# Two feed-forward layers on one core: the first product taken for pairs of batch elements in seven blocks of products

## The chip, the cores and the metric

The kernel runs on one NeuronCore of a Trainium2 chip, as one launch. The metric is the time of one execution on the device in microseconds (us); the time before is the median of five runs. All arithmetic is in 32-bit floats.

## The reference, cut to what matters

A sequence of two transformer blocks over 16 batch elements of 256 tokens with 256 features. Each block has a self-attention, a cross-attention and a feed-forward layer, each added to its input, with a layer norm modulated by a condition ahead of it. Only the feed-forward layers are changed:

```
# layer 0 (x: 16 x 256 x 256; ff_w1: 256 x 1024; ff_w2: 1024 x 256)
ffn_in = _adaln(x, cond, ln2_w, ln2_b, g2_w, g2_b, b2_w, b2_b)
h = jax.nn.gelu(ffn_in @ ff_w1 + ff_b1, approximate=False)
x = h @ ff_w2 + ff_b2 + x
# layer 1, the same with other weights
h = _ln(x, ln3_w, ln3_b) * (1 + sc3[:, None, :]) + sh3[:, None, :]
x = x + jax.nn.gelu(h @ W1 + b1, approximate=False) @ W2 + b2
```

Layer 0's attentions have 16 heads of 64 columns with rotary embedding, layer 1's 16 heads of 16 columns.

## The kernel before

There are six phases (self-attention, cross-attention and feed-forward of layer 0, then of layer 1) of 16 jobs, one for each batch element. An attention job has two steps `s`, a feed-forward job four. One loop over all steps issues everything; with `manual_schedule` the order in which the code issues is the order in which each engine (PE, DVE, ACT, POOL, and SP for the DMAs) works. An instruction that has to wait holds up everything behind it on its engine. PSUM is one tile, `banks`, of eight banks, and the code names the bank of each product.

A matrix product of 128 output rows is a call of `product` (line 82 in the profile): four matmuls of 32 output rows each, which lie on different columns of the array. Each such matmul instruction leaves two records in the profile.

**Preparing an input.** `prepare_moments` (mean and variance on DVE, lines 321 to 325, then `rstd` on POOL, line 327), `prepare_norm` (normalisation and 32x32 transposes on DVE, lines 335 and 345; four DMAs on SP that write `turned` to DRAM, line 350; then two bias additions on POOL, line 420), `prepare_fetch` (four DMAs that read `fetched` back transposed, line 360), `prepare_input` (`affine`: one half of the modulation on ACT, line 393, the other on POOL, line 394). These run one to three jobs ahead of the job that needs them.

**First product.** `ffn_hidden(job, u)` does a quarter of `ffn_in @ w1` in each of its four steps: two 128-row chunks of the 1024 hidden features, for each two products over the 256 input features and 256 tokens, so 16 products for each element, then two gelus on ACT straight from PSUM (line 701).

**Second product.** It is already done by Strassen's seven products. `fold_weights` (line 724, five additions of 128x512) makes sums of blocks of the second weight, once for each phase. `fold_inner` (line 733, five additions of 128x512) makes sums of blocks of the hidden values. `finish_folded` does seven products of 128x128 blocks over 512 features, 28 calls of `product` with 128 columns, into two banks, and adds them to `x` on DVE (lines 747 to 754). Folds of the element before come in step 0, its `finish_folded` in step 2. For layer 0's last elements, whose results are finished beside layer 1's first attention jobs, `finish` does the plain second product (addition on line 772). Layer 0's attentions end in the same folded way.

**Around the feed-forward phases.** The first job of a feed-forward phase also ends the last attention job: in layer 0 `sum_up` (sums of the softmax, reciprocal on line 609) and `scale` on POOL (line 624), in layer 1 `normalize` (reciprocal on line 677, shuffles on line 685, two multiplications on POOL, line 686) and `finish`. `fold_weights` comes in step 1 of this first job. At the end of the kernel the last element is folded and finished alone. `look_outside`, `judge` and `count_outside` read back all softmax sums, test their range and choose whether a general version has to run as well; on these inputs it does not.

Of the kernel before, what the change touches and what calls it, by code (L numbers as in the profile page):

```python
# [10 lines left out]
F32 = mybir.dt.float32  # L11
# [32 lines left out]
def fast(ctx: ExitStack, tc: tile.TileContext, a: dict, out: bass.AP, flag):  # L44
# [6 lines left out]
    assert NB >= 11  # L51
# [19 lines left out]
    turn_of_ffn = [1]  # L71

    def next_bank():
        turn_of_ffn[0] = (turn_of_ffn[0] + 1) % 8
        return turn_of_ffn[0]

    def product(out, lhsT, rhs, start, stop):


        for g in range(4):  # L80
            cut = slice(32 * g, 32 * g + 32)
            nc.tensor.matmul(out[cut], lhsT[:, cut], rhs, start=start, stop=stop)  # L82
# [307 lines left out]
    def affine(pt, cw, scale, bias, tag, name, eng=nc.gpsimd):  # L390

        dst = work.tile([cw, 2, N], F32, tag=tag, name=name)
        nc.scalar.activation(dst[:, 0, :], pt[:, 0, :], AF.Identity, bias=bias(0), scale=scale(0))
        eng.tensor_scalar(dst[:, 1, :], pt[:, 1, :], scale(1), bias(1), ALU.mult, ALU.add)
        return dst
# [41 lines left out]
    def prepare_input(job):  # L437

        b, key = job["b"], job["key"]
        factor, addend = job["phase"]["mod"]  # L440
        job["hT"] = hT = affine(
            job.pop("hraw"), P,
            lambda c: factor[:, c, b : b + 1], lambda c: addend[:, c, b : b + 1], "hT", f"hT_{key}",
            nc.vector if b == 0 and job["p"] == 0 else nc.gpsimd,
        )
        if not job["cross"]:
            job["kT"] = hT
        elif job["layer"] == 0:
            job["kT"] = affine(
                job.pop("craw"), P,  # L450
                lambda c: column("L0_xcond_ca_lnc_w", c), lambda c: column("L0_xcond_ca_lnc_b", c),
                "cT", f"cT_{key}",
            )
# [191 lines left out]
    def layer1_sums(job, c, e, at):  # L645

        key, v, prs = job["key"], job["v"], job["pr"].pop(2 * c + e)
        o = bank(at, N)
        for t in range(NT):
            for h in range(4):  # L650
                nc.tensor.matmul(  # L651
                    o[32 * h : 32 * h + 32], v[:, t, 4 * c + h, 32 * e : 32 * e + 32],
                    prs[h // 2][:, h % 2, t, :], start=(t == 0), stop=(t == NT - 1),
                )

        if c == 0 and e == 0:
            job["parts"].append(work.tile([P, 4, N], F32, tag="part", name=f"oT_{key}", bufs=4)[:, 0:2, :])
            job["sums"] = work.tile([P, N], F32, tag="inv", name=f"sums_{key}")  # L660
        raw, sums = job["parts"][0][:, c, :], job["sums"]
        if e == 0:
            nc.scalar.activation(raw, o, AF.Copy, scale=mask[:, 0:1])
        else:
            nc.vector.scalar_tensor_tensor(raw, o, mask[:, 1:2], raw, ALU.mult, ALU.add)
        eighth = mask[:, 4 - 2 * e + c : 5 - 2 * e + c]
        if c == 0 and e == 0:
            nc.scalar.activation(sums, o, AF.Copy, scale=eighth)
        else:
            nc.vector.scalar_tensor_tensor(sums, o, eighth, sums, ALU.mult, ALU.add)  # L670
# [17 lines left out]
    def ffn_hidden(job, u):  # L688
        w, key = job["phase"]["w"], job["key"]
        ph = bank(next_bank(), 2, N)  # L690
        if u % 2 == 0:
            job["halves"].append(work.tile([P, 4, N], F32, tag="part", name=f"g_{key}_{u}", bufs=4))
        g = job["halves"][-1][:, 2 * (u % 2) : 2 * (u % 2) + 2, :]
        for c in range(2):
            for k in range(KC):
                product(
                    ph[:, c, :], w[f"w1{u // 2}"][:, k, (2 * (u % 2) + c) * P : (2 * (u % 2) + c + 1) * P], job["hT"][:, k, :],
                    k == 0, k == KC - 1,
                )
        for c in range(2):  # L700
            nc.scalar.activation(g[:, c, :], ph[:, c, :], AF.Gelu, bias=column(w["b1"], 2 * u + c))  # L701
        job["parts"].append(g)
# [32 lines left out]
    def finish_folded(job, at):  # L735

        x, weights, hidden = xs[job["b"]], job["phase"]["folded"], job.pop("folded")
        hurry = len(at) == 3
        first, second, third = (bank(i, 4, P) for i in (at if hurry else (*at, at[1])))
        places = {5: first[:, 0], 2: first[:, 1], 4: first[:, 2], 3: first[:, 3],  # L740
                  1: third[:, 0], 7: second[:, 1], 6: second[:, 2]}
        for m in (3, 6, 4, 5, 2, 1, 7) if hurry else places:
            for c in range(4):
                product(places[m], hidden[m][:, c, :], weights[m][:, c, :], c == 0, c == 3)
# [8 lines left out]
        nc.vector.tensor_tensor(outer, third[:, 0:1, :].to_broadcast([P, 2, P]), outer, ALU.add)  # L753
# [22 lines left out]
    def look_outside():  # L776

        worst = const.tile([P, 2], F32, name="worst")
        every = wtile([P, 4 * NB * 16 * N // P], "wv", "every")
        nc.sync.dma_start(out=every, in_=sums_seen.rearrange("(p n) h r q -> p (n h r q)", p=4 * NB)  # L780
                          .rearrange("p (s m) -> (p s) m", s=P // (4 * NB)))
        return worst, every

    def judge(worst, every):
        nc.vector.tensor_reduce(worst[:, 0:1], every, AX.X, ALU.add)
        nc.vector.tensor_reduce(worst[:, 1:2], every, AX.X, ALU.min)
        nc.vector.tensor_scalar(within[:, 0:1], worst[:, 0:1], SUM_HIGH, None, ALU.is_le)
        nc.vector.tensor_scalar(within[:, 1:2], worst[:, 1:2], 1.0 / SUM_HIGH, None, ALU.is_ge)

    def count_outside():  # L790

        pw = bank(next_bank(), 2)[0:1]
# [107 lines left out]
    prepare_input(jobs[1])  # L900
    for i, (j, s) in enumerate(steps):
# [5 lines left out]
        late = prev if not ffn else jobs[j - 2] if prev["kind"] == "ffn" else None  # L907
# [4 lines left out]
        if s == 1 and job["b"] == (3 if ffn else 1) and more:  # L912
# [12 lines left out]
        if ffn and layer0 and job["b"] in (2, 5, 8):  # L925
            at = phases[3 + job["b"] // 3]
            if s == 0:
                at["make_mod"] = at["mod_load"]()
            if s == 3:
                make_mod = at  # L930
        if ffn and layer0 and job["b"] in (3, 6, 9) and s == 3:
            at = phases[2 + job["b"] // 3]
# [5 lines left out]
        if ffn:  # L938
            ffn_hidden(job, s)
            if s == 1 and prev["kind"] == "attn" and layer0:  # L940
                sum_up(prev, next_bank())
            if s == 2 and prev["kind"] == "attn" and not layer0:
                finish(prev, next_bank())
            if prev["kind"] == "ffn":
                if s == 0:
                    fold_inner(prev, nc.vector, 5, 2, 1, 7, 6)
                if s == 2:
                    finish_folded(prev, (next_bank(), next_bank()))
            then = attention(i + 2, 1)
            if s == 2 and then:  # L950
                stage_a(then[0], 0, next_bank())
            if s == 0 and prev["kind"] == "attn" and prev["layer"] == 1:
                normalize(prev)
            if late is not None and s == 3:
                finish(late, next_bank())
            if s == 2 and then:
                for t in range(NT):
                    layer1_values(then[0], next_bank(), t)
            if make_mod:
                make_mod["mod"] = make_mod["make_mod"](next_bank())  # L960
            if s == 1 and after is not None:
                prepare_fetch(after)
            if s == 1 and third is not None:
                prepare_moments(third)
                prepare_norm(third)
            if s == 1 and prev["kind"] == "attn":
                fold_weights(job["phase"])
            if s == 3 and after is not None:
                prepare_input(after)
            if s == 3 and prev["kind"] == "attn" and layer0:  # L970
                scale(prev)
        elif layer0:
            then = attention(i + 1, 0)
            stage_t(job, 2 * s, 0)
# [21 lines left out]
            if late is not None and s == 1:  # L996
                if then:
                    finish_folded(late, (4, 5))
# [12 lines left out]
            else:  # L1011
                prepare_norm(third)
                prepare_context(third)
                prepare_input(after)
                if job["b"] == 0:
                    fold_weights(job["phase"])
        else:
# [14 lines left out]
            if s == 0:  # L1032
                prepare_moments(third)
            else:
                prepare_norm(third)
                prepare_input(after)
        scores(i + 1)
        if job["last"] and s == 0 and job["b"] in (2, 6):
            seen_sums = look_outside() if job["b"] == 2 else count_outside()
        if job["last"] and s == 3 and job["b"] == 3:  # L1040
            judge(*seen_sums)
    fold_inner(jobs[-1], nc.vector, 6, 5, 2, 1, 7)
    finish_folded(jobs[-1], (1, 2, 3))
# [615 lines left out]
```

## Time and profile before

| | |
|---|---|
| median of five runs | 2200.36 us (2198.2 to 2200.98) |
| the profiled execution | 2201.28 us, span 2199.5 us |
| granted TensorE clock | 0.999 |
| PE busy | 2184.5 us (99%) |
| DVE busy | 1662.4 us (76%) |
| POOL busy | 1072.1 us (49%) |
| ACT busy | 839.1 us (38%) |
| feed-forward phase of layer 0 on PE | 1293.85 to about 1533 us |
| feed-forward phase of layer 1 on PE | 1982.2 to 2192 us |

A line of the profile's groups names the line of code, the engine, the operation, the output and input tiles, the shape and the count; then busy time in us and the mean of one instruction in ns; then the idle time of that engine just before, with what ended it. In a timeline the columns are the start and the duration in us, and the idle time before stands in brackets with what ended it. PEld is the loading of weights, which runs beside PE; SPq are the DMAs that SP issues. The records of matmuls overlap four deep, so the pace of PE is read from the starts of groups, not from the mean of one record. The slices of the page are a fortieth of the span, 55 us each.

### The profile page before, as it was taken

What the parts mean: (1) busy time and instruction counts of PE and PEld (TensorE: products, weight loads), DVE (VectorE), ACT (ScalarE), POOL (GpSimd) and SP (SyncE); (2) the same over time, 40 slices, a digit from 0 to 9 for tenths busy, and PEclk for the clock granted to TensorE, in tenths of its full rate; (3) what the DMA queues carried; (4) which work ended last, traced back from release to release, by engine and by line L of the source; (5) the groups of instructions that cost most, each with busy time, mean ns of one, the idle gap of its engine ahead of it and who ended that gap; (6) DMA issues with size and microseconds to landing.
All of it is one profiled execution on the core that took longest, in us unless ns stands there. A gap on an engine that the chain in (4) does not pass through costs nothing.

```text
span 2199.5 us, 110711 instructions
## 1 busy us (share of the span) xinstructions
PE 2184.5 (99%) x50469; PEld 1438.7 (65%) x50469; DVE 1662.4 (76%) x3119; ACT 839.1 (38%) x1306; POOL 1072.1 (49%) x1036
## 2 busy tenths in 40 slices
PE   9999999999999999999999999999999999999998
PEld 5666666666665666666666668786656556557887
DVE  5886777777788898889898876664777777777654
ACT  3323323323223323333333332334666666663322
POOL 3766656656657867676776752221323232222220
PEclk9999999999999999999999999999999999999999
DMA  6110111110132221212212033221222232223221
GB/s 192 46 39 22 25 40 23 24 41 22 27 85 72 68 63 35 55 46 43 57 36 60 23 74 87 52 45 29 62 42 42 55 92 59 62 52 85 61 63 36
DMA packets 307975, 117.78 MB, mean 54 GB/s; under 512 B 244308, under 2 KB 290728, under 8 KB 307368
## 3 DMA queue, kind: packets, MB, share of 16 engines
q1 hardware_dynamic: 307496, 110.61, 21.4%
q8 instruction: 397, 6.50, 1.3%
q14 instruction: 82, 0.67, 0.1%
HBM read 77.14 MB, written 33.29 MB: 50 GB/s over the span
## 4 chain that ended last, share of the span: by engine, by line
PE 93%; POOL 2%; DVE 2%; issue 1%; DMA 1%; SPq 1%; ACT 0%; DVEq 0%; POOLq 0%; ACTq 0%
PE banks L82 61%; PE banks L566 15%; PE banks L635 9%; PE banks L651 5%; PE banks L502 1%; PE banks L469 1%; POOL raw L624 1%; DVE m L523 1%; POOL qk L531 1%; DMA spread<-sums_seen 0%; POOL folded L733 0%; PE banks L186 0%; DMA sums_seen<-inv 0%; SPq L615 0%; PE banks L198 0%
## 5 line engine op out<-in xcount | busy, mean ns | idle before, releaser
L578 ACT ACTIVATE pr<-banks 128x1024 f32<-128x1024 f32 x576 | 487.5, 937 | 413.1 <-PE banks L566 208.6
L531 POOL TENSOR_TENSOR qk<-m,m 128x512 f32<-128x512 f32 x256 | 347.4, 1377 | 302.4 <-DVE m L523 205.3
L523 DVE TENSOR_TENSOR m<-banks,rope 128x512 f32<-128x512 f32 x512 | 324.2, 679 | 84.6 <-POOL qk L531 77.2
L587 DVE TENSOR_TENSOR both<-pr 128x512 f32<-128x512 f32 x256 | 221.5, 878 | 108.0 <-ACT pr L578 107.6
L642 ACT COPY raw<-banks 128x512 f32<-128x512 f32 x128 | 75.2, 587 | 472.4 <-PE banks L635 452.9
L566 PE MATMUL banks<-qk 32*64 32x256 f32 x8192 | 240.6, 377 | 2.9 <-DVE x L750 1.9
L635 PE MATMUL banks<-pr,v 128*32 128x256 f32 x4096 | 233.2, 379 | 0.0
L566 PEld LDWEIGHTS banks<-qk 32*64 32x64 f32 x8192 | 184.4, 131 | 63.2 <-issue 22.2
L701 ACT ACTIVATE g<-banks,cols 128x256 f32<-128x256 f32 x256 | 107.2, 471 | 288.3 <-PE banks L82 275.0
L635 PEld LDWEIGHTS banks<-pr,v 128*32 128x32 f32 x4096 | 133.0, 110 | 88.5 <-ACT pr L578 0.7
L82 PE MATMUL banks<-folded_w,folded 128*32 128x128 f32 x5856 | 174.6, 273 | 0.3 <-POOL folded L733 0.2
L624 POOL TENSOR_TENSOR raw<-raw,spread 128x512 f32<-128x512 f32 x128 | 163.0, 1306 | 21.0 <-DMA spread<-sums_seen 21.0
L82 PEld LDWEIGHTS banks<-folded_w,folded 128*32 128x32 f32 x5856 | 162.6, 110 | 0.9 <-POOL folded L733 0.8
L593 DVE STREAM_TRANSPOSE squares<-both 128x1024 f32<-128x1024 f32 x128 | 159.4, 1246 | 4.4
L600 DVE TENSOR_REDUCE rows<-squares 128x32 f32<-128x1024 f32 x128 | 155.5, 1215 | 2.2
L686 POOL TENSOR_TENSOR oT<-oT,spread 128x256 f32<-128x256 f32 x64 | 45.8, 736 | 209.6 <-DVE spread L685 209.6
L327 POOL TENSOR_TENSOR rstd<-ve,neg_half 128x2 f32<-128x2 f32 x95 | 73.6, 774 | 144.1 <-DVE ve L325 140.8
L82 PE MATMUL banks<-hT,wk_sa 128*32 128x256 f32 x2048 | 135.6, 383 | 0.0
L651 PE MATMUL banks<-pr,wide_v 128*32 128x256 f32 x2048 | 134.4, 379 | 1.1 <-ACT pr L578 1.1
L420 POOL TENSOR_TENSOR x<-x,bo_b 128x256 f32<-128x256 f32 x96 | 73.2, 782 | 127.2 <-DVE xh L335 127.2
L82 PE MATMUL banks<-hT,wq_sa 128*32 128x256 f32 x2048 | 134.0, 379 | 0.0
L82 PE MATMUL banks<-hT,wq_ca 128*32 128x256 f32 x2048 | 133.9, 379 | 0.0
(157 smaller groups left out, 3677.9 us busy)
## 6 DMA issues: line engine op xcount, KB each, us to landing
turned<-blocks SPq DMA_DIRECT2D x380, 64.0 KB
fetched<-turned SPq DMA_DIRECT2D x380, 64.0 KB
spread<-sums_seen SPq DMA_DIRECT2D x128, 128.0 KB
x<-in_x SPq DMA_DIRECT2D x16, 256.0 KB
fetched_c<-turned_c SPq DMA_DIRECT2D x64, 64.0 KB
cT<-in_ctx_turned SPq DMA_DIRECT2D x16, 256.0 KB
out<-x SPq DMA_DIRECT2D x16, 256.0 KB
ctx<-in_ctx SPq DMA_DIRECT2D x16, 192.0 KB
```

What stands on the lines that cost most here:

```text
L82: nc.tensor.matmul(out[cut], lhsT[:, cut], rhs, start=start, stop=stop)
L523: nc.vector.tensor_tensor(m, pq, rope[:, s : s + 1, :].to_broadcast([P, 2, N]), ALU.mult)
L531: nc.gpsimd.tensor_tensor(r, x, y, (ALU.subtract, ALU.add)[out])
L566: nc.tensor.matmul(banks[64 * g : 64 * g + 64, at + h, t * N : (t + 1) * N], lhs, rhs, start=(half == 0), stop=(half == 1 or job["layer"] ...
L578: nc.scalar.activation(pr[:, one], sc[:, one], AF.Exp, scale=0.125 if job["layer"] == 0 else 0.25)
L587: nc.vector.tensor_tensor(job["both"][:, 2 * p : 2 * p + 2, :], pr[:, :, 0, :], pr[:, :, 1, :], ALU.add)
L593: nc.vector.transpose(job["squares"].rearrange("p b k -> p (b k)"), job.pop("both").rearrange("p h n -> p (h n)"))
L600: nc.vector.tensor_reduce(job["rows"][:, u, :], job.pop("squares"), AX.X, ALU.add)
L624: nc.gpsimd.tensor_tensor(part, part, spread[:, u : u + 1, :].to_broadcast([P, 2, N]), ALU.mult)
L635: nc.tensor.matmul(o[32 * h : 32 * h + 32, half, :], v[:, t, col : col + 32], prs[h // 2][:, h % 2, t, :], start=(t == 0), stop=(t == NT - 1),
L651: nc.tensor.matmul(o[32 * h : 32 * h + 32], v[:, t, 4 * c + h, 32 * e : 32 * e + 32], prs[h // 2][:, h % 2, t, :], start=(t == 0), stop=(t ...
L701: nc.scalar.activation(g[:, c, :], ph[:, c, :], AF.Gelu, bias=column(w["b1"], 2 * u + c))
```

## The change

Feed-forward elements are taken in pairs. A pair's inputs are one tile `pair`, and its eight steps are q = 0 to 7. The first product of a pair becomes a product of 2x2 blocks (halves of the hidden features of one weight tile by halves of the 256 input features; input features by halves of the tokens), done with seven block products instead of eight. One block product is four calls of `product` with 2 x 128 columns, the same 128 tokens of both elements.

`split_weights` makes four sums of weight blocks on POOL, once for each phase, in the last attention job of layer 0 and in job 4 of layer 1's cross-attention. `split_input` makes four sums of input blocks on POOL for each pair. The sums on the output side are formed partly by letting PE add to banks that are still kept, partly by copies of a bank on ACT (`kept`) and additions on DVE (`join`). The gelus are 24 for each pair: eight of 256 columns in place in SBUF, eight of 128 columns in SBUF, eight of 128 columns from PSUM. Of the five folds of an element, three are on DVE and two on POOL. `finish_folded` of the pair before comes at q = 2 and q = 4 (at 7 in the last pair), with its products in another order.

`enter_ffn` prepares more inputs ahead of a feed-forward phase: it splits the first pair's input and does the norms of elements 2 and 3. `fold_weights` moves from the first element's step 1 to q = 3 of the first pair, behind its `ffn_hidden`. In layer 0 the elements 14 and 15 are both finished by the plain product beside layer 1's first attention jobs, and at the end of the kernel the elements 14 and 15 are folded and finished one after the other. `judge` works on two halves and comes later, `count_outside` has a fixed bank, and the steps at which the next phases' modulations are made are moved.

```diff
+    def split_weights(ph):
...
+        nc.gpsimd.tensor_tensor(s1, a[1][0], a[1][1], ALU.add)
+        nc.gpsimd.tensor_tensor(s2, s1, a[0][0], ALU.subtract)
+        nc.gpsimd.tensor_tensor(s3, a[0][0], a[1][0], ALU.subtract)
+        nc.gpsimd.tensor_tensor(s4, a[0][1], s2, ALU.subtract)
...
+    def split_input(job, part):
...
+        if part == 0:
+            nc.gpsimd.tensor_tensor(t1, b[0][1], b[0][0], ALU.subtract)
+            nc.gpsimd.tensor_tensor(t2, b[1][1], t1, ALU.subtract)
+        else:
+            nc.gpsimd.tensor_tensor(t[:, 0], b[1][1], b[0][1], ALU.subtract)
+            nc.gpsimd.tensor_tensor(t[:, 1], b[1][0], t2, ALU.subtract)
...
-    def ffn_hidden(job, u):
...
+    def ffn_hidden(job, q):
...
+        main, other, side = (2 + 2 * odd, 4 - 2 * odd, 6)
...
+        if q == 0:
...
+            block(main, a[0][0], b[0][0], True)
+            job["first"] = kept("both", 0)
+            if pending:
+                gelu(pending[0], 0, every_token)
+                fold(pending[0])
+            block(side, s1, job["split"][0], True)
+            if pending:
+                block(other, a[0][1], b[1][0], True)
+                join(0, 0, other, job.pop("first"))
+        elif q == 1:
+            block(main, s2, job["split"][1], False)
+            second = kept("squares", 1)
+            if pending:
+                job["second"] = second
+                gelu(pending[1], 0, every_token)
+            else:
+                block(0, s4, b[1][1], True)
+                join(0, 1, 0, second)
+                for e, one in enumerate((job, mate)):
+                    sums = one["halves"][0][:, :, second_half]
+                    nc.vector.tensor_tensor(sums, parted(side)[:, :, e, :], sums, ALU.add)
+        elif q == 3:
+            if pending:
+                fold(pending[1])
+            block(main, s3, job["split"][2], False)
+            third = []
...
+            join(1, 1, side, third)
+            for one in (job, mate):
+                gelu(one, 1, second_half)
+        elif q == 5 and pending:
+            block(side, s4, b[1][1], False)
+            join(0, 1, side, job.pop("second"))
+        elif q == 5:
+            block(other, a[0][1], b[1][0], True)
+            join(0, 0, other, job.pop("first"))
+        elif q == 6:
+            block(main, a[1][1], job["split"][3], False)
...
+            for e, one in enumerate((job, mate)):
+                gelu(one, 1, first_half, parted(main)[:, :, e, :])
...
+    def enter_ffn(j):
+        prepare_input(jobs[j + 2])
+        for part in range(2):
+            split_input(jobs[j + 1], part)
+        prepare_norm(jobs[j + 3])
+        prepare_moments(jobs[j + 4])
+        prepare_norm(jobs[j + 4])
...
+            q = s + 4 * (job["b"] % 2)
+            if q in (0, 4) and third is not None and (previous or q == 4):
+                prepare_moments(third)
+            for ahead in ((after,) if previous else (after, third)) if q == 0 else (third,) if q == 3 and previous else ():
+                if ahead is not None:
+                    prepare_fetch(ahead)
+            if q == 0 and not previous and before["layer"] == 1:
+                normalize(before)
...
+            ffn_hidden(one, q)
+            if previous:
+                if q in (2, 7 if one["b"] == NB - 2 else 4):
+                    finish_folded(jobs[one["index"] - (2 if q == 2 else 1)], (0, 1), (4, 3, 2, 5, 1, 6, 7))
+            else:
+                if q == 1 and layer0:
+                    sum_up(before, 5)
+                if q == 2 and not layer0:
+                    finish(before, 5)
+                if q == 3:
+                    fold_weights(job["phase"])
...
+            ahead = {2: after, 4: after} if previous else {1: after, 3: third}
+            if ahead.get(q) is not None:
+                prepare_input(ahead[q])
+            if q in (4, 6) and nxt is not None and nxt["kind"] == "ffn":
+                split_input(nxt, q // 6)
...
-    fold_inner(jobs[-1], nc.vector, 6, 5, 2, 1, 7)
-    finish_folded(jobs[-1], (1, 2, 3))
+    for n in (2, 1):
+        fold_inner(jobs[-n], nc.vector, 2, 1, 6, 5, 7)
+        finish_folded(jobs[-n], (2 * n - 4 + 4 * (n == 1), 2 * n - 3 + 4 * (n == 1)), (4, 3, 2, 5, 1, 6, 7))
```

## The prediction

> **What bounds the kernel now.** I read the page's busy shares and slices first.
>
> ```profile
> PE 2184.5 (99%) x50469; PEld 1438.7 (65%) x50469; DVE 1662.4 (76%) x3119; ACT 839.1 (38%) x1306; POOL 1072.1 (49%) x1036
> ...
> PE   9999999999999999999999999999999999999998
> ...
> DVE  5886777777788898889898876664777777777654
> ACT  3323323323223323333333332334666666663322
> POOL 3766656656657867676776752221323232222220
> ...
> PE 93%; POOL 2%; DVE 2%; issue 1%; DMA 1%; SPq 1%; ACT 0%; DVEq 0%; POOLq 0%; ACTq 0%
> ```
>
> PE never idles, at a granted clock of 0.999, and its work is 93% of the chain. So removed PE work is time, unless PE then waits. The feed-forward stages (slices 24 to 28 and the last four or so) have DVE at about 65%, ACT 33%, POOL 22%: room for other work. Next, the timeline of layer 1's stage, PE lines of three elements:
>
> ```profile
> 2132.75 7.10 PE L82 MATMUL banks<-hT,w_b 128*32 128x256 f32 x128
> ...
> 2145.77 7.10 PE L82 MATMUL banks<-hT,w_b 128*32 128x256 f32 x128
> ...
> 2152.67 1.94 PE L82 MATMUL banks<-w_b,folded 128*32 128x128 f32 x64
> ...
> 2158.79 7.10 PE L82 MATMUL banks<-hT,w_b 128*32 128x256 f32 x128
> ```
>
> An element takes 2145.77 − 2132.75 = 13.02 us: 6.90 for the first product (128 records, 53.9 ns each; a `product` call is 8 records, 0.43 us) and 6.12 for the folded second one (2152.67 to 2158.79, 224 records, 27.3 ns each). Nothing stalls. The groups, shapes apart, price the other engines:
>
> ```profile
> L701 ACT ACTIVATE g<-banks,cols 128x256 f32<-128x256 f32 x256 | 107.2, 471 | 288.3 <-PE banks L82 275.0 <-ACT hT L393 12.4 <-ACT g L701 0.9
> L531 POOL TENSOR_TENSOR qk<-m,m 128x512 f32<-128x512 f32 x256 | 347.4, 1377 | 302.4 <-DVE m L523 205.3 <-PE banks L82 96.3 <-DVE add_a L173 0.7
> L733 DVE TENSOR_TENSOR folded<-g,g 128x512 f32<-128x512 f32 x93 | 58.6, 684 | 37.3 <-ACT g L701 37.3
> L733 POOL TENSOR_TENSOR folded<-raw,raw 128x512 f32<-128x512 f32 x90 | 128.3, 1454 | 2.4
> L642 ACT COPY raw<-banks 128x512 f32<-128x512 f32 x128 | 75.2, 587 | 472.4 <-PE banks L635 452.9 <-POOL qk L531 19.5
> ```
>
> Last, the timeline where layer 0 enters its feed-forward stage:
>
> ```profile
> 1294.48 0.69 DVE L772 TENSOR_TENSOR x<-banks,x 128x512 f32<-128x512 f32 x1 [1.48 <-PE banks L82]
> ...
> 1301.65 3.64 DVE L724 TENSOR_TENSOR folded_w<-w_a 128x512 f32<-128x512 f32 x5
> 1302.85 2.51 SPq L360 DMA_DIRECT2D fetched<-turned  x4
> ...
> 1307.08 0.60 ACT L393 ACTIVATE hT<-fetched,add_a,fac_a 128x256 f32<-128x256 f32 x1 [4.78 <-DMA fetched<-turned]
> ```
>
> PE runs through here now, but a fetch takes 4.2 us from first issue to its reader and `fold_weights` holds DVE for 3.64.
>
> **PE work removed.** A pair's first products become 7 blocks × 4 products × 8 records × 53.9 ns = 12.07 us instead of 2 × 6.90 = 13.80. Sixteen pairs: −1.73 × 16 = −27.6. Element 14 of layer 0's stage now ends in layer 1's attention with the unfolded product, 128 records of 53.9 ns = 6.90 instead of 6.12: +0.8. PE **−26.8 us**. The right operand becomes two stretches of 128 columns; no row shows that, and I take the 256-column price, since PE's records elsewhere follow the columns (27.3 for 128, 53.9 for 256). Were each stretch to pay its own few ns, say 1 ns on each of 3,584 block records, it would be +4.
>
> **Steady pair, 24.31 us if PE never waits.** PE order from 0: main 1.73, side 3.45, other 5.18, main 6.90, finish of the previous pair's first element 13.02, main 14.75, finish of its second 20.87, side 22.59, main 24.31.
> - ACT: two copies of 128x1024 at about 1.0 (the 1024-wide exponential L578 has 1.035), two of 512 at 0.59, an affine 0.6 twice, 24 gelus. A 256-column gelu goes at 0.42 (two in 0.84 in the timeline). For 128 columns there is no row: L578 falls from 1.035 to 0.595 for 512 fewer elements, 0.86 ns an element, so 0.42 − 0.11 = 0.31; at worst 0.42, no gain from size. 8 × 0.42 + 16 × 0.31 = 8.3; in all 12.7 of 24.3.
> - DVE: six folds 0.68, joins 4 × 0.69 + 4 × 0.42, adds behind the finishes 2 × 2.4, two moments and norms 2 × 2.8: about 19.5 (80%).
> - POOL: four folds at 1.3 to 1.45, four `split_input` adds at 0.75 (as L686, 0.736), biases 2 × 1.5, affines, rstd: about 14.
>
> Due times: other at 3.45 writes the banks from which the previous pair's last 8 gelus read. The first of them can start about 1.0 before the pair ends (its product is one of the last block's four), so at a pace g they end near −1.0 + 8g, and not before 1.9: 2.4 at 0.42. Folds on POOL end near 8.0 and 9.4, wanted at 9.5 and 12.1. `join(0,1)` ends before side is rewritten at 26.0. The split inputs are there 2.5 us early. So I cost the steady pair at **0**, bounds 0 and +1.0 a pair.
>
> [...]
>
> [...]
>
> **Entry to layer 0's stage.** Before it PE has no stall. Now POOL, behind the raw scale that ends near 1287.8, does rstd, `split_weights` (four of 1.38 to 1.5), the affine and the first `split_input`s (4 × 0.75, to 1297.6) and a bias, and reaches element 3's rstd only near 1300; its norm on DVE ends 1301.8, and `join(0,1)` with the two `sums` (4 × 0.69) and `sum_up`'s reciprocal follow to 1304.7. PE has four blocks from 1293.85 (6.90), `sum_up` (0.46) and one block: 1302.9. "other" writes bank 5, which the reciprocal reads: wait 1.8. On SP, element 2's fetch stands behind element 3's four `turned` issues (2.6, from 1301.8), so starts at 1304.4; plus 4.2 it lands near 1308.4. ACT's affine of it stands ahead of the third copy (0.6 a half): the first half is done 1309.4. The last main block, ready at 1306.4, waits 3.0 for that and ends 1311.1. DVE's queue then holds `join(1,1)` (to 1311.3), `fold_weights` (3.64), moments (1.25) and only then `join(0,0)` (1.4): 1317.4. Pair 1's first block writes the banks that this join reads: wait 6.3. Together **+11.1**, bounds +5 (fetch lands before the copy is due, only part of the weights' fold in the way) and +15 (each POOL step at its contended length).
>
> **Entry to layer 1's stage.** Its split weights lie in a POOL gap of 6.7 us in cross-attention job 4 and need 5.5: 0, up to 2 if the gap moves. PE does four blocks from 1982.22 to 1989.1 and wants the last attention's `oT`. DVE, after norm 2 (1984.5), now has element 3's moments 1.25, rstd's wait 0.8 and norm 1.5 ahead of the reciprocal (1.71) and shuffles (0.9): 1990.6; POOL's first half 0.72: 1991.3. Wait 2.2, where 0.7 stood before (the two waits on `oT` there). After finish and three blocks PE is at 1998.2; `join(1,1)` ends 1998.0, and weights' fold, moments and `join(0,0)` (3.64 + 1.25 + 1.4) take DVE to 2004.3: wait 6.1. **+7.6**, bounds +3 and +10.
>
> **End.** Now: from the last first product (2186.45) to the end of the run 13.05 us, 6.12 of it PE. After: two elements are left, 18.36 of PE (a block and both finishes count from there) in 27.5, since DVE does all ten folds and element 15's stand behind 14's adds. 9.1 beyond PE instead of 6.9: **+2.2**, bounds 0 and +4.
>
> **Layer 0 to 1.** PE waits for DVE's adds of element 13 on bank 1 and ACT's gelu backlog and table load; it waited 1.7 to 2.2 before. **+0.7**, bounds −0.5 and +2.
>
> Edits at nothing: `judge` in halves and later (4 × 1.215 on DVE at one place, in a pair with 4.8 free; 0, at worst 3 once, a pair late by the queue behind it); modulation moved by steps, `count_outside` on another bank, new pool tags (0 to 1).
>
> **Sum.** 2201.28 − 26.8 + 11.1 + 7.6 + 2.2 + 0.7 = 2196.1 on the profiled run, which is 0.9 over the median of the runs: **2195.2**, −0.23%. A measurement of this kernel tells about 0.2% (4.4 us) from no change, so the line is at 2196.0 and 2204.8.
>
> **Rivals.**
> A. The sum as it stands, 0.45. Own range 2189 to 2201, by moving each entry's half way to its bounds. About 0.25 of it lies under 2196.0, 0.20 above.
> B. The entries hide their chains, 0.22: POOL reaches rstd early (at the raw scale's end 1287.8 it has a gap), so element 2's fetch is issued before element 3's, and M4's wait goes; each entry costs about 5 and 3, the sum 2184. For it: 2184 to 2190, faster. Against: `fold_weights` stands ahead of the join in the written order whatever POOL does.
> C. ACT's gelus set the pair, 0.22: place, "other" at 3.45. It decides where 8g − 1.0 passes 3.45, at g = 0.56. At 0.68 the wait is 1.0 in each of 14 pairs, 2195.2 + 14 = 2209, slower; 2205 to 2212. For it: gelus of 128 columns, half of them in place in SBUF, have no row, and an activation from SBUF (L393, 0.60 for 256) is dearer than the gelu from PSUM (0.47). Against: 0.56 for 128 columns is more than 0.42 for 256.
> D. The entries cost their upper bounds, 0.11: 2195.2 + 3.9 + 2.4 = 2201.5, with 0.06 under 2204.8 and 0.05 over it.
> That the block form saves no PE records is excluded: the written order has 192 fewer matmuls of 256 columns and 112 fewer of 128 (−192 × 2 × 53.9 ns − 112 × 2 × 27.3 ns = −26.8 us).
>
> Chances: faster 0.25 + 0.22 = 0.47; same 0.20 + 0.06 = 0.26; slower 0.22 + 0.05 = 0.27. The range 2184 to 2208 leaves out perhaps 0.11 in C and 0.06 in B.
>
> **What would show it.** Right: PE lines of a pair 24.3 us apart in both stages; PE waiting once about 6 us for a DVE join behind L724 at each entry, and for an ACT copy behind the affine in layer 0; 27 us from the last block to the end. Wrong: ACT or POOL as releaser of PE inside every pair (C); entries without PE gaps (B); block records dearer than 53.9 ns.

## The result and the profile after

The changed kernel takes 2202.66 us (median of 28 runs, 2199.23 to 2206.10) against 2199.12 for the kernel before (48 runs). The ratio is 1.0016, interval 1.0011 to 1.0021: no change by the 0.2% of the forecast, and on the slow side of it. In the set where the changed kernel stood once more beside other versions it was 1.0024 (1.0015 to 1.0033). The forecast was 2195.2, faster by 0.23%.

The page of the changed kernel, busy shares, slices, granted clock and chain:

```profile
span 2198.7 us, 109886 instructions
...
PE 2165.3 (98%) x49861; PEld 1429.0 (65%) x49861; DVE 1730.9 (79%) x3190; ACT 911.1 (41%) x1498; POOL 1211.5 (55%) x1164
...
PE   9999999999999999999999989999999999998998
...
PE 92%; DVE 3%; POOL 2%; DMA 1%; issue 1%; SPq 0%; ACT 0%; DVEq 0%; POOLq 0%; ACTq 0%
```

PE's busy time is down by 19 us, not by 26.8, and DVE has grown from 2% to 3% of the chain. The first slice with an 8 is the entry to layer 0's feed-forward phase, the next the entry to layer 1's, the last the end. The profiled execution took 2200.49 us at a mean granted clock of 0.997; over the other runs the clock was 0.994 to 0.997, and 0.999 or 1.0 in every run of the kernel before.

Between those places the change does what it says. PE's lines of two pairs, layer 1:

```profile
2028.96 2.05 PE L76 MATMUL banks<-hT,w_b 128*32 128x256 f32 x32
...
2053.28 2.05 PE L76 MATMUL banks<-hT,w_b 128*32 128x256 f32 x32
```

Their starts are 24.32 us apart; the forecast said 24.31. At the entry to layer 0's phase the timelines of PE, ACT and DVE read (bracket: idle before, and what ended it):

```profile
1306.89 0.60 ACT L387 ACTIVATE hT<-fetched,add_a,fac_a 128x256 f32<-128x256 f32 x1 [7.71 <-DMA fetched<-turned]
1307.40 1.05 ACT L817 COPY kept<-banks 128x512 f32<-128x512 f32 x2
...
1308.06 3.25 PE L76 MATMUL banks<-split,w_a 128*32 128x256 f32 x32 [4.21 <-POOL hT L388]
...
1309.49 3.09 DVE L859 TENSOR_TENSOR folded_w<-w_a 128x512 f32<-128x512 f32 x5
...
1313.57 1.28 DVE L769 TENSOR_TENSOR g<-banks,kept 128x512 f32<-128x512 f32 x2
...
1314.99 3.20 PE L76 MATMUL banks<-hT,w_a 128*32 128x256 f32 x32 [3.68 <-DVE g L769]
...
1318.00 1.92 PE L76 MATMUL banks<-split,split_a 128*32 128x256 f32 x32
...
2002.27 3.64 PE L76 MATMUL banks<-hT,w_b 128*32 128x256 f32 x32 [4.38 <-DVE g L769]
```

The last line is the same second wait at the entry to layer 1. Both forecast waits are there: the block behind the copy that stands behind the affine and its fetch (the bracket names POOL's half of the same affine, which ended about then), and the second pair's block behind the join that stands behind the folds of weights. But the two blocks behind the waits take 3.25 and 3.20 us where such a block takes 1.92. The windows view gives the reason; columns are the stretch, its length, PE's busy time and instructions, the granted clock, DMA share and GB/s:

```profile
1300.00:1304.00 4.00, 3.58 (x61) 1.00 0.38 61
1304.00:1307.30 3.30, 0.00 (x0) 1.00 0.49 132
1307.40:1310.70 3.30, 2.64 (x28) 0.50 0.30 89
1310.80:1314.00 3.20, 0.52 (x11) 1.00 0.39 104
1314.20:1317.50 3.30, 2.51 (x24) 0.50 0.01 2
1317.60:1321.00 3.40, 3.40 (x68) 1.00 0.50 81
2000.40:2007.00 6.60, 4.74 (x48) 0.50 0.16 26
```

A stretch of about 3.4 us in which PE worked for nothing or for only 0.52 us is followed by one at half the clock, twice here, and in layer 1 the half clock lasts 6.8 us. The forecast has no term for this. Another thing it lacked is in the last pair:

```profile
2165.36 2.10 DVE L868 TENSOR_TENSOR folded<-g,g 128x512 f32<-128x512 f32 x2
2167.38 0.68 DVE L868 TENSOR_TENSOR folded<-g 128x512 f32<-128x512 f32 x1
2167.98 1.41 DVE L769 TENSOR_TENSOR g<-banks,kept 128x256 f32<-128x256 f32 x4
...
2169.11 1.93 PE L76 MATMUL banks<-hT,split_b 128*32 128x256 f32 x32 [2.91 <-DVE g L769]
```

In other pairs the finish of the previous pair's second element (6.12 us) lies between; in the last pair it comes only at q = 7, so nothing covers DVE's folds and join.

### The profile page after: what moved, and what is told of

The parts are those of the page before. It is cut to its first block, busy times and chain, and to the rows that moved or that the text cites. A ratio compares the mean times of both kernels' runs of the same rounds, so it can differ in the third digit from the quotient of the medians.

```text
span 2198.7 us, 109886 instructions
## 1 busy us (share of the span) xinstructions
PE 2165.3 (98%) x49861; PEld 1429.0 (65%) x49861; DVE 1730.9 (79%) x3190; ACT 911.1 (41%) x1498; POOL 1211.5 (55%) x1164
## 4 chain that ended last, share of the span: by engine, by line
PE 92%; DVE 3%; POOL 2%; DMA 1%; issue 1%; SPq 0%; ACT 0%; DVEq 0%; POOLq 0%; ACTq 0%
PE banks L76 59%; PE banks L567 16%; PE banks L636 9%; PE banks L652 5%; PE banks L503 1%; PE banks L470 1%; POOL raw L625 1%; DVE m L524 0%; POOL folded L868 0%; DVE g L769 0%; DVE folded L868 0%; DMA spread<-sums_seen 0%; DMA sums_seen<-inv 0%; POOL qk L532 0%; DVE folded_w L859 0%
## 5 line engine op out<-in xcount | busy, mean ns | idle before, releaser
L588 DVE TENSOR_TENSOR both<-pr 128x512 f32<-128x512 f32 x256 | 228.5, 905 | 106.7 <-ACT pr L579 106.3
L625 POOL TENSOR_TENSOR raw<-raw,spread 128x512 f32<-128x512 f32 x128 | 165.3, 1325 | 21.9 <-DMA spread<-sums_seen 19.3
L567 PE MATMUL banks<-q,k 32*64 32x256 f32 x4096 | 129.2, 382 | 1.5 <-issue 1.0
L476 ACT COPY v<-banks 128x512 f32<-128x512 f32 x128 | 70.4, 593 | 143.3 <-PE banks L76 81.7
```

Source lines behind the costliest of these rows:

```text
L567: nc.tensor.matmul(banks[64 * g : 64 * g + 64, at + h, t * N : (t + 1) * N], lhs, rhs, start=(half == 0), stop=(half == 1 or job["layer"] ...
L588: nc.vector.tensor_tensor(job["both"][:, 2 * p : 2 * p + 2, :], pr[:, :, 0, :], pr[:, :, 1, :], ALU.add)
L625: nc.gpsimd.tensor_tensor(part, part, spread[:, u : u + 1, :].to_broadcast([P, 2, N]), ALU.mult)
```

## The experiments

Two theories were set against each other. *Clock*: a long wait of PE costs more than its length, since PE then works at half clock. *Waits only*: the miss is in the lengths of waits that I mis-sized or overlooked.

**The clock by itself: delays in the kernel before.** Unused DVE work ahead of the folds of some elements of layer 1's feed-forward phase.

```diff
                 if s == 0:
+                    if not layer0 and job["b"] in range(4, 12):       # gap_long: (4, 6, 8, 10)
+                        for _ in range(9):                            # gap_long: 13
+                            nc.vector.tensor_tensor(scratch, scratch, scratch, ALU.mult)
                     fold_inner(prev, nc.vector, 5, 2, 1, 7, 6)
```

Eight short ones:

> The kernel before, with 9 further additions' worth of DVE work (128x512 multiplications of a scratch tile, 0.68 us each, result unused) ahead of the folds of eight elements (4 to 11) of layer 1's feed-forward phase. They delay the folds by 6.1 us, of which about 3.4 were slack, so PE should wait about 2.7 us eight times, 21.6 us in all. Clock theory (a wait that leaves PE idle for a whole window of about 3.4 us halves its granted clock for the next one): no wait here fills a window, so the granted clock stays 0.999 and the time is before + about 22 = 2221. Rival (only the lengths of waits count): the same 2221. A clock under 0.998 here would speak against the 3.4 us.

Four long ones:

> The kernel before, with 13 of the same unused DVE multiplications ahead of the folds of four elements (4, 6, 8, 10) of layer 1's feed-forward phase: 8.8 us each, so waits of PE of about 5.4 us, four times, 21.6 us in all, as much as with eight short ones. Clock theory: most of the four waits hold a whole idle window, so each is followed by 3.4 or 6.8 us at half clock, 1.3 to 3 us more: granted clock 0.995 to 0.997 and 5 to 12 us more than the short ones, 2226 to 2233. Rival (only the lengths of waits count): as the short ones, 2221 within 2.

And the four long ones with PE kept busy:

```diff
+        if job["last"] and job["b"] in (3, 5, 7, 9):
+            w = job["phase"]["w"]["w10"]
+            for _ in range(18 if job["b"] == 3 else 9):
+                product(banks[:, at[0], 0:N], w[:, 0, 0:P], w[:, 0, 0:N], True, True)
         for m in (3, 6, 4, 5, 2, 1, 7) if hurry else places:
```

> The kernel before with the four long delays of DVE (13 unused multiplications ahead of the folds of elements 4, 6, 8 and 10), and with unused products of PE ahead of the delayed second products: 18 in the first place, where PE waited 8.6 us, 9 in the three others, where it waited 4.2 to 4.3. The folds come when they came, so the waits keep their ends, but PE is busy in them. Clock theory: the granted clock goes back to 0.999 and the time is 31 - 21.3 = 10 us under that of the four long delays, ratio to the kernel before about 1.0095. Rival (a block behind a wait is slow for another reason, such as cold operands or the start of PE's queue): as the four long delays, 1.0139.

| | ratio to before (interval) | PE's waits | granted clock |
|---|---|---|---|
| eight short | 1.0115 (1.0099 to 1.0130) | 5.69 once, else 1.35 to 2.45; 19.2 in all | 0.997 |
| four long | 1.0139 (1.0123 to 1.0154) | 8.59, 4.22, 4.26, 4.27; 21.3 in all | 0.994 |
| four long, filled | 1.0101 (1.0086 to 1.0116) | 0.83, 0.34, 0.37, 0.37 | 0.999 or 1.0 |

The four long delays cost 0.0139 × 2199.4 = 30.6 us where PE was idle for 21.3; with PE busy in the same delays they cost 22.2. So the half clock is 8.4 us here, some 2 us a wait, though the two intervals leave this open by some 5 us either way. The trace says the same without them: behind the four waits PE works for 3.05, 5.21, 2.90 and 5.13 us at a granted clock of 0.50, 16.3 in all; it takes about twice as long so (3.64 us for a block of 1.95), and some 8.1 of that is lost. The rival falls: a block is not slow because it follows a wait, but because PE was idle in it. The first element's wait was longer than meant, since the test of the sums is on DVE just there (4.6 us, ahead of the added work). The eight short delays cost 25.3 us for 19.2 of waits; work at half clock explains 3.4 of the difference, and the rest is within the interval. My 3.4 us as the length that matters fell as well. PE's lines of one long wait, of the same place with PE kept busy (0.83 of its wait left), of one short wait that was followed by a slow block, and of the next, that was not:

```profile
2043.83 3.42 PE L82 MATMUL banks<-w_b,folded 128*32 128x128 f32 x64 [8.59 <-DVE folded L733]
...
2042.68 1.95 PE L82 MATMUL banks<-w_b,folded 128*32 128x128 f32 x64 [0.83 <-DVE folded L733]
...
2086.64 3.22 PE L82 MATMUL banks<-w_b,folded 128*32 128x128 f32 x64 [2.45 <-DVE folded L733]
...
2102.89 1.95 PE L82 MATMUL banks<-w_b,folded 128*32 128x128 f32 x64 [1.35 <-DVE folded L733]
```

A wait of 2.45 us was enough once; of the six others of 1.35 to 2.11 none was followed by half clock, and all five of 4.2 and more were, for 3.4 or 6.8 us.

Of two waits of nearly the same length one was followed by half clock and the other not. The wait for the last attention in layer 1 is 2.07 us in the second trace of the changed kernel and 2.08 in the first. In the first trace the clock changes at 1307.38, 1310.79, 1314.20, 1317.62, 2000.28 and 2007.11 us, whole multiples of 3.41 us apart, and the lines cut both traces into stretches of that length, counted from their own changes. In the second trace (the first two lines) one stretch holds 2.13 us without work of PE, and half clock follows; in the first trace (the last three) the idle time is shared by two, 1.61 and 0.53 us, and the clock stays at 1.00. The columns are as above:

```profile
1990.09:1993.50 3.41, 1.28 (x24) 1.00 0.51 83
1993.50:1996.91 3.41, 3.41 (x36) 0.50 0.57 128
...
1986.63:1990.04 3.41, 1.80 (x36) 1.00 0.50 80
1990.04:1993.45 3.41, 2.88 (x52) 1.00 0.52 117
1993.46:1996.87 3.41, 3.41 (x72) 1.00 0.32 90
```

Nor does length alone tell among longer ones: in the second trace waits of 2.85 and 3.29 us were followed by half clock and one of 3.80 was not, nor was the 2.91 of the last pair in the first. Every measured wait of 3.84 us or more that is named here was followed by it.

**The clock in the changed kernel.** Unused products in the three longest waits at the entries, then in all five long waits:

```diff
+            if q == 6 and not previous and layer0:
+                fill(job["phase"], 8)
+            if q == 0 and job["b"] == 2:
+                fill(job["phase"], 9)                                 # first version: 7, and only these two places
...
+                    fill(job["phase"], 4, 5)                          # ahead of finish(before, 5) in layer 1
...
+            if mate["b"] == NB - 1:
+                fill(ph, 6)                                           # ahead of the last pair's side block
```

> The changed kernel, with products whose result is not used (into bank 0) put where PE waits longest: 8 of 256 columns (3.45 us) ahead of the first pair's last block in layer 0, 7 (3.0 us) ahead of the second pair's first block in both layers. Nothing that the waits are for is touched, so the waits keep their ends. Clock theory: PE is no longer idle for a window, the granted clock goes back to about 0.998 or 0.999, and the blocks behind the waits take 1.73 us instead of 3.0: 5 to 8 us less than the changed kernel, 2195 to 2198. Rival (only the lengths of waits count, the slow blocks have another cause, such as operands that come late): no change, 2202 to 2203, or slower if the filling runs over.

> The changed kernel once more, unaltered, so that the others of this set stand beside it on the same chip. Both theories: 1.001 to 1.002 times the kernel before, granted clock 0.994 to 0.997.

> The changed kernel with unused products in all of its long waits: 8 ahead of the first pair's last block in layer 0, 9 ahead of the second pair's first block in both layers, 4 ahead of the last attention's finish in layer 1, 6 ahead of the last pair's block that waits for DVE. The waits keep their ends. If the half clock behind the waits is what the forecast lacked, the granted clock is 0.999 in every run and the time 4 to 8 us under the changed kernel beside it. If it is only the small part that the first filling gave (1.8 us in the medians), 1 to 3 under, and most of the miss lies in the waits themselves.

The first version gave 1.0008 (0.9999 to 1.0017) at clocks of 0.997 to 1.0: some waits were left. With all filled the clock is 0.999 or 1.0 in all eleven runs, and the ratio 1.0004 (0.9995 to 1.0013) beside the unaltered kernel's 1.0024 at a mean of 0.995: 0.0020 × 2199.4 = 4.4 us, with intervals that all but touch. That is less than (0.9996 − 0.9949) × 2200 = 10 us, the most the lower clock could take. One reason shows in the filled kernel:

```profile
1309.15 1.93 PE L76 MATMUL banks<-split,w_a 128*32 128x256 f32 x32 [0.73 <-POOL hT L388]
...
1316.08 1.93 PE L76 MATMUL banks<-hT,w_a 128*32 128x256 f32 x32 [1.12 <-DVE g L775]
```

Both blocks are at full speed, yet they start 6.93 us apart, as in the kernel unfilled (1308.06 and 1314.99): the slow first block was covered by the next wait, which DVE ends.

**The two queues at the entries.** Folds of weights behind the join, and element 2's affine behind the copy, each alone and together:

```diff
-                if q == 3:
+                if q == 5:                                            # late
                     fold_weights(job["phase"])
...
-            ahead = {2: after, 4: after} if previous else {1: after, 3: third}
+            ahead = {2: after, 4: after} if previous else {3: third}  # aff
+            if q == 3 and not previous:
+                prepare_input(after)
```

> The changed kernel, with fold_weights at q = 5 behind join(0,0) instead of at q = 3 ahead of it, in both layers. My queue reading (second pair's first block waits for the join behind 3.0 us of weight folds on DVE): that wait falls from 3.68 to about 0.6 us in layer 0 and from 4.38 to about 1.4 in layer 1, 6.1 us less. With the clock theory the half clock behind these two waits goes too, 1.3 and 3.0: about 10 us less, 2192 to 2193, and a granted clock of 0.997 to 0.998, since the wait of 4.2 for the copy stays. Without it 6 less: 2196 to 2197. Rival (the join waits for something else, such as the copy or the affine): no change.

> The changed kernel, with element 2's affine (prepare_input) put behind the third copy and the gelus on ACT in the first pair (q = 3 instead of q = 1), both layers. Queue reading: in layer 0 the last block no longer waits 4.2 us for a copy that stands behind the affine and its fetch. But the second pair's first block still waits for the join behind fold_weights, which can start about 3.7 us earlier: that wait becomes about 5. So 3.5 to 4 us less from the waits, and with the clock theory one window at half clock (1.3) less or none, since one wait of 5 stays: 2197 to 2199. Layer 1: no change. Rival (the last block waits for the split input or the bank, not for the copy): no change, 2202 to 2203.

> The changed kernel, with fold_weights behind join(0,0) and element 2's affine behind the third copy. Queue reading: layer 0's entry then waits only about 2 us for the join and about 1 to 2 for the second pair's split inputs (their fetch lands near 1309), instead of 8.2; layer 1's as with fold_weights alone. About 7 to 8 us less from the waits; with the clock theory no window is idle in layer 0 either and 4 to 6 more: 2188 to 2191, granted clock 0.998 or 0.999. Without the clock: 2194 to 2196.

PE's lines of the wait that was aimed at, in layer 0, with the folds late, with the affine late and with both:

```profile
1313.99 1.93 PE L76 MATMUL banks<-hT,w_a 128*32 128x256 f32 x32 [1.28 <-ACT hT L387]
...
1309.34 3.38 PE L76 MATMUL banks<-hT,w_a 128*32 128x256 f32 x32 [3.84 <-DVE g L769]
...
1307.19 3.64 PE L76 MATMUL banks<-hT,w_a 128*32 128x256 f32 x32 [3.54 <-ACT hT L387]
```

Folds of weights late: 1.0000 (0.9991 to 1.0009), 3.5 us under the changed kernel instead of 10. The waits on the join went, from 3.68 to 1.28 and from 4.38 to 1.57, but both now end with ACT's `hT`: the pair's fetched inputs are next. Part was given back behind them: in layer 0 PE waits 2.5 us for POOL's scaling (`raw`), because POOL had not got further, and in layer 1 about 1 us inside the second pair's folded products, for which the trace names no releaser. Its trace also has half clock in three places still, behind waits of 4.07, 2.08 and 2.90.

Affine late: 0.9990 (0.9981 to 0.9999), 5.7 under. The wait of 4.21 is gone and the one for the join is 3.84, better than the expected 5.

Both: 0.9982 (0.9973 to 0.9991), 7.5 under the changed kernel and already under the kernel before. What is left of layer 0's entry is a wait of 3.5 to 3.9 us for the pair's inputs.

**The end.** The last pair's folds behind its join, and the last folds in the order in which they are wanted:

```diff
-            if pending:
+            if pending and mate["b"] != NB - 1:
                 fold(pending[1])
...
             join(1, 1, side, third)
+            if mate["b"] == NB - 1:
+                fold(pending[1])
...
-        fold_inner(jobs[-n], nc.vector, 2, 1, 6, 5, 7)
+        fold_inner(jobs[-n], nc.vector, 2, 5, 1, 6, 7)
```

> The changed kernel, with two orders on DVE changed at the end: in the last pair the folds of element 13 come behind join(1,1) instead of ahead of it, and the two last elements' folds come in the order 2, 5, 1, 6, 7 that their products ask for. Queue reading: the wait of 2.91 us in the last pair falls to about 1.2, the two of 0.72 to nothing: 3.1 less, 2199 to 2200. With the clock theory nothing more, or up to 1.3 where the wait of 2.9 had filled a window. Rival (the last pair's wait is for the copy or for the block before it): 1.4 less.

1.0001 (0.9992 to 1.0010), 3.3 us under: the wait fell from 2.91 to 1.57 and the two of 0.72 went.

```profile
2168.62 1.93 PE L76 MATMUL banks<-hT,split_b 128*32 128x256 f32 x32 [1.57 <-DVE g L769]
```

**All three.**

> The changed kernel with all three moves: fold_weights behind join(0,0), element 2's affine behind the third copy, the two orders at the end. If the waits at the entries, the half clock behind them and the waits at the end are all that took the gain, the sum of the parts: 2185 to 2188, 11 to 14 us less than the kernel before. If the clock has no part: 2191 to 2193.

2189.51 us, ratio 0.9964 (0.9950 to 0.9977): 7.9 us under the kernel before and 11.4 under the changed one, by the ratios that each has to the kernel before beside it. That is a version that beats both, but less than the 11 to 14 expected; layer 0's entry still has this (POOL, ACT and PE):

```profile
1306.21 2.90 POOL L388 TENSOR_SCALAR hT<-fetched,fac_a,add_a 128x256 f32<-128x256 f32 x2 [6.85 <-DMA fetched<-turned]
...
1308.06 0.60 ACT L387 ACTIVATE hT<-fetched,add_a,fac_a 128x256 f32<-128x256 f32 x1 [1.33 <-DMA fetched<-turned]
...
1308.72 3.64 PE L76 MATMUL banks<-hT,w_a 128*32 128x256 f32 x32 [3.92 <-DVE folded_w L861]
```

The bracket names the folds of weights, which PE does not read before q = 2. This block reads the half of the inputs that ACT makes, and what ends with PE's start is ACT's affine of element 3, at 1308.66, behind its fetch; POOL's half ends only at 1309.1, behind PE's start. The block behind runs at half clock again (3.64).

**One step further.** To move that fetch, the norm of element 2 one step earlier:

```diff
                 prepare_moments(third)
+                if nxt["kind"] == "ffn":
+                    prepare_norm(third)
...
     def enter_ffn(j):
-        prepare_norm(jobs[j + 3])
+        prepare_fetch(jobs[j + 3])
```

> The version with the three moves (folds of weights behind the join, element 2's affine behind the copy, the two orders at the end), and the norm of element 2 now made one step earlier, beside the last attention job, so that its fetch is not issued behind element 3's four writes. What is left at the entries is a wait of 3.92 in layer 0 and 2.06 in layer 1 for the affines of elements 2 and 3, and 2.08 for the last attention's result. Queue reading: element 3's writes and fetch come 1.5 to 3 us earlier, so the first falls to about 1 and its half clock goes, the second to about 0, the third to about 1: 7 to 9 us less than the version with three moves, about 0.993 of the kernel before. Rival (DVE is so full beside the last attention job that the earlier norm delays the attention): 0.995 to 0.997.

0.9987 (0.9978 to 0.9996): the rival, and worse than its range; the version with three moves is 5 us faster. PE's waits at the entry, now ahead of and inside the first pair:

```profile
1295.28 1.93 PE L76 MATMUL banks<-hT,w_a 128*32 128x256 f32 x32 [1.74 <-ACT hT L387]
1299.91 2.37 PE L76 MATMUL banks<-split,split_a 128*32 128x256 f32 x40 [1.84 <-DVE x L908]
...
1312.48 2.54 PE L76 MATMUL banks<-hT,w_a 128*32 128x256 f32 x32 [2.30 <-ACT hT L387]
```

The wait for the pair's inputs fell from 3.92 to 2.30, but the earlier norm pushed back the last attention's addition and the first inputs, 1.74 + 1.84. Together that is 2 us more than the 3.92 before; what makes up the other 3 was not taken apart.

## Why the prediction was wrong

By the profiled execution, in its own terms:

| term | forecast | in the trace | with all waits filled |
|---|---|---|---|
| a steady pair | 24.31 | 24.32 | |
| waits inside pairs | 0 | 0.35 once, behind `judge` | 0.36 |
| entry, layer 0 | +11.1 | +11.4 | +10.8 |
| entry, layer 1 | +7.6 | +8.8 | +7.5 |
| last pair's wait | no term | +2.9 | +2.9 |
| end | +2.2 | +2.6 | +2.7 |
| layer 0 to 1 | +0.7 | about +1.9 | |

The entries are measured from the first block to the first folded product, less the PE work in between: 37.73 − 26.33 in layer 0, and 30.22 − 20.70 in layer 1, less 0.7 that was there before. The end is 27.8 us from the last block to the end of the run (forecast 27.5).

*The step that failed* is the price of a wait: "wait 6.3", "wait 3.0", "wait 6.1" stand in the sum at their lengths, while a long wait also costs clock. As waits the two entries were right: 18.3 us with the clock kept, against 18.7. The clock came on top, and differently from run to run. The last pair's wait, for which the sum had no term at all, is the second step that failed. The profiled execution had a light case (0.997) and gained 0.8 us on that of before. In the others the clock was mostly 0.995, and they took 2.2 us more, while the profiled run of before was itself 2.2 above its median. Against the kernel before by medians the miss is 0.0016 + 0.0023 = 0.0039, or 8.6 us. Beside the filled kernel it was 0.0024 + 0.0023, or 10.3 us. Of these 4.4 is the clock, by the filled kernel; of the 5.9 that stay with the clock kept, 2.9 is the last pair's wait, 1.2 the change of layers, 0.5 the end and 0.4 the wait behind `judge`, less 0.4 at the entries, all by the trace, and some 1.3 stays open. Each ratio is good to about 2 us either way, so this names the causes, and neither their order nor the last microsecond; the change of layers no run took apart.

*Single waits were less right than their sum*, so that the sum of the entries came out is in part luck. In layer 0 "other" waited 0.27 and not 1.8, since the first half of that block goes to bank 4, which the reciprocal does not read. The wait for the copy was 4.21 and not 3.0. The join came 22.5 us after the first block and not 23.6, half of it since `fold_weights` took 3.09 us there, not the 3.64 of the trace of before; of the forecast wait of 6.3 for it, 3.68 was left, or 5.2 with PE at full speed ahead of it (1309.15 + 1.73 to 1316.08 in the filled kernel). Each wait had the releaser that was named: with one queue taken away, the named work was late no more and something else was.

*The last pair*: the part on the end started to count at the last block. The move of the finish to q = 7 was read, but its price was looked for only behind it, where it fills PE, and not ahead of it, where 6.12 us of cover are gone.

*Rivals.* B (entries hide their chains) did not hold; the two moves that make it partly true were worth 7.5 us. C was not it: eight gelus of 128 columns in SBUF take 2.45 us, 0.306 each by the busy time of their group (forecast 0.31, deciding from 0.56), and no steady pair waits for ACT. D, entries at their upper bounds, is nearest in size, 2201.5, but its place for the excess, each POOL step of the entry at a contended length, no run shows: at the changed kernel's entry to layer 0 the affines on POOL take 0.56 us each, the sums of input blocks 0.73 to 0.79 and the sums of weight blocks 1.29 to 1.62. One longer step stands in the trace of before: the affine at 1307.16 took 1.57 us beside two folds on DVE, where the median of its group is 0.56. That the clock could change had no place among the rivals, for a kernel whose clock had been 0.999.

```profile
L732 ACT ACTIVATE g<-g,cols 128x128 f32<-128x128 f32 x128 | 39.2, 388 | 21.5 <-DVE g L769 21.5
```

## What to carry to other kernels

Where the bound engine is PE, price a new wait of some 4 us or more at its length and about 2 us on top (the four of 4.22 to 8.59 us lost some 8.1 to half clock), unless another wait behind it covers that; one between 2 and 4 us may cost the same on top or not (2.07 was followed by half clock, 3.80 was not), and shorter ones cost only themselves (behind 1.35 the block took its 1.95 us). Look for such waits where a steady pattern begins and ends: a gain in each of sixteen rounds was eaten by one queue order at either entry and one in the last round, and orders alone, with the same work, brought 11.4 us of it back. When an order is mended, name who is late next before counting the gain.

## What the runs showed of the hardware that was not expected

- The half clock needs no wait of 3.4 us: one of 2.07 was followed by it, one of 2.08 was not. It lasted 3.4 or 6.8 us behind a single wait. Keeping PE at unused products through the long waits prevented it: 0.999 or 1.0 in all fifteen runs of the two fully filled kernels.
- A fold on DVE and a fold or scaling on POOL take turns. The groups of the changed kernel, one fold beside POOL's scaling, and one with POOL idle:

```profile
L868 DVE TENSOR_TENSOR folded<-g,g 128x512 f32<-128x512 f32 x62 | 60.3, 1010 | 25.9 <-ACT g L732 25.9
L868 POOL TENSOR_TENSOR folded<-g,g 128x512 f32<-128x512 f32 x28 | 42.6, 1520 | 20.4 <-ACT g L732 11.4 <-PE banks L76 8.3
...
1318.71 5.91 POOL L625 TENSOR_TENSOR raw<-raw,spread 128x512 f32<-128x512 f32 x4
...
1323.41 1.77 DVE L868 TENSOR_TENSOR folded<-g 128x512 f32<-128x512 f32 x1
...
1340.67 0.67 DVE L868 TENSOR_TENSOR folded<-g 128x512 f32<-128x512 f32 x1
```

The same DVE addition took 684 ns in the kernel before. The mean of 1010 hides two sizes: of the 94 folds on DVE 62 take 0.64 to 0.69 us, and 32 take 0.84 to 1.78, each of which ends 0.55 us behind the end of a fold (L868) or a scaling (L625) that was running on POOL when it started. So such a fold waits for the end of POOL's instruction. The forecast had a contended length only for POOL's steps. It cost a steady pair nothing (24.32 us); in the last pair two folds take 2.10 us instead of 1.28 ahead of the join that PE waits for, some 0.8 of those 2.91.
